# Marking the slots of a node: a clamp on GpSimd and an equality on VectorE in place of a distance on ScalarE and a comparison

## The chip, the cores and the metric

The kernel runs on one core of a Trainium2 chip. The metric is the device time of one launch in microseconds (us). Before the change the median of three runs is 543.99 us (543.93 to 545.51).

## The reference

One layer of a message-passing network over 128 graphs of 64 nodes with 128 features each. The adjacency matrix of a graph is symmetric, has ones on its diagonal and is sparse otherwise.

```python
f_i, f_j = x[:, :, None, :], x[:, None, :, :]                 # all pairs of nodes of a graph
m   = mlp(concat(f_i, f_j), msg weights)                      # 3 layers, relu and layernorm twice
agg = sum(m * adj[..., None], axis=2)
out = x + mlp(concat(x, agg), upd weights)                    # 3 layers, relu and layernorm twice
# mlp: h = layernorm(relu(x@w0 + b0)); h = layernorm(relu(h@w1 + b1)); return h@w2 + b2
```

## The kernel before

**Edges, not pairs.** Only pairs with an edge are worked on. Two graphs form a pair `p` (64 of them) whose nodes fill the 128 partitions; each graph gets `CAP` = 640 slots, one for each of its edges, in the order of the nodes. Four pairs form a block `b` (16 of them). Ten chunks of 512 edges go with a block, 160 in all.

**Node marks, the part that is changed.** A node of the pair (a partition) owns the slots from its start to its end, both running counts of edges. `place` (`place_first` for block 0) works out the counts: `before` is the start, `cum` the end, `mid` their sum. `slot` is a constant row 1, 3, 5, ... 1279 in 16-bit floats, so that a slot belongs to a node where |slot - mid| is less than the node's degree `deg`. Two functions make the marks: `distance(p)` writes `D[p]`, the absolute difference, on ScalarE, and `make_tp(p)` compares it with `deg` on VectorE and writes `TP[p]`, a matrix of 0 and 1, 128 x 640, in 16-bit floats. `D` has two buffers, `TP` eight. `node_rows(p)` widens `TP[p]` to 32 bits (on GpSimd from pair 6 on), `marks` and `compare` make a second matrix for the other end of each edge, `stack` puts both into `S` by DMAs of SP's queue, and `node_marks` turns `TP[p]` by another DMA.

**The edge layers.** For chunk `n`, `layer0(n)` gathers the first layer's sums by TensorE: the one-hot matrix `S` against the rows `ab` of the nodes, which are held as a high and a low part, so each piece takes two matmuls. A chunk of 512 slots overlaps one or two graphs of 640 slots: `pieces(n)` gives pieces of 512; 128 and 384; 256 and 256; 384 and 128; 512 in turn, in the order of the slots. ScalarE applies relu. `stats0` transposes the chunk into a PSUM bank (`hT`) and VectorE takes its statistics by bn_stats. `seed(n)` writes bias times standard deviation into the PSUM bank `z` of the chunk (two banks, `n % 2`), on VectorE for chunks with `n % 10` in 3, 4, 8 and on ScalarE in four pieces otherwise; `layer1(n)` adds its matmuls onto it, ScalarE applies relu, and `stats1` takes statistics again. `weights` (GpSimd) and `reduce` (TensorE) sum the edges of each node.

**The update.** Once in a block a `Unit` does the second mlp on 512 nodes. `bias0(u)` makes its first bias, `deg * c2u + ub0b`, by four VectorE instructions of 128 columns; `residual` (`xo`) and `upd_shift` (`usdb`) are GpSimd's, `layer_out` and `finish` VectorE's.

**Order.** It is written out by hand. `at(n, place, fn, ...)` files a step under iteration `n` and a place in it; the last loop runs the iterations, in each the places "a", "m", then layer 1, layer 0 and the transposes, "k", `stats1`, and the places "x" to "e". Each engine works its own instructions strictly in that order. Layer 1 of chunk `m` is in iteration `m + 8`. For pair `p`, whose slots begin in chunk `n = 2.5 p`, the distance is filed under `n - 7`, `make_tp` under `n - 6`, `node_rows` under `n - 5`, `stack` under `n - 4`. `bias0` is filed under the first iteration of its unit, four iterations ahead of its use by `layer_out`. The first three pairs are made before the loop, `distance(0)` between `place_first` and `place_pair(0)`.

Of the kernel before, what the change touches and what calls it, by code (L numbers as in the profile page):

```python
# [9 lines left out]
F32 = mybir.dt.float32  # L10
F16 = mybir.dt.float16
F32R = mybir.dt.float32r
I32 = mybir.dt.int32
AF = mybir.ActivationFunctionType
ALU = mybir.AluOpType
# [9 lines left out]
def tile_gnn(  # L25
# [40 lines left out]
    nc = tc.nc  # L66
    B, N, C = x.shape
    P = 128
    assert C == P and N == 64
    CAP = 640  # L70
# [9 lines left out]
    PB = 4  # L80
# [84 lines left out]
    slot = const.tile([P, CAP], F16, name="slot")  # L165
# [9 lines left out]
    W = {}  # L175
# [62 lines left out]
    def bc(t, n, axis=1):  # L238

        s = [P, n, C] if axis == 1 else [P, C, n]  # L240
        return t.unsqueeze(axis).to_broadcast(s)
# [60 lines left out]
    def edge_path(es):  # L302
        adp = es.enter_context(tc.tile_pool(name="adp", bufs=2))
        tpp = es.enter_context(tc.tile_pool(name="tpp", bufs=8))
# [35 lines left out]
        def at(n, place, fn, *args):  # L340
            plan.setdefault((n, place), []).append((fn, args))

        def run(n, place):
            for fn, args in plan.pop((n, place), ()):
                fn(*args)

        blocks = {b: {} for b in range(NB)}
        TP, S, H, ST0, V0, Y, ST1, Q, OH, WT, YS, MK, D, IR, JR, SR, Z = ({} for _ in range(17))
# [38 lines left out]
        def whole(b, eng):  # L387
            cum = cumall[:, b * PB:(b + 1) * PB]
            eng.tensor_scalar(cum, blocks[b].pop("raw"), WHOLE, WHOLE, op0=ALU.add,
                              op1=ALU.subtract)  # L390
            return cum
# [6 lines left out]
        def place(b):  # L398

            blk = blocks[b]  # L400
            cum = whole(b, nc.gpsimd)
            before = adp.tile([P, PB], F32, name="before")
            nc.gpsimd.tensor_tensor(before, cum, blk["deg"], op=ALU.subtract)
            blk["mid"] = adp.tile([P, PB], F32, name="mid")
            nc.gpsimd.tensor_tensor(blk["mid"], cum, before, op=ALU.add)
            pos = adp.tile([P, PB, N], F32, name="pos")
            nc.gpsimd.tensor_tensor(pos, blk.pop("rk"),
                                    before.unsqueeze(2).to_broadcast([P, PB, N]), op=ALU.add)
            blk["pos"] = pos
# [9 lines left out]
        def place_first():  # L419
            blk = blocks[0]  # L420
            rk = blk["rk"]
            cum = whole(0, nc.vector)
            before = blk["before"] = adp.tile([P, PB], F32, name="before")
            nc.vector.tensor_tensor(before, cum, rk[:, :, N - 1], op=ALU.subtract)
            blk["mid"] = adp.tile([P, PB], F32, name="mid")
            nc.vector.tensor_tensor(blk["mid"], cum, before, op=ALU.add)

        def place_pair(q):
            blk = blocks[0]
            for g in range(2):  # L430
                s = slice(g * N, (g + 1) * N)
                nc.vector.scalar_tensor_tensor(posall[s, 0, q, g, :], blk["rk"][s, q],
                                               blk["before"][s, q:q + 1], blk["an"][s, q],
                                               op0=ALU.add, op1=ALU.mult)
# [61 lines left out]
                del blk["ab_ps", half]  # L496


        def distance(p):
            b, q = divmod(p, PB)  # L500
            D[p] = tpp.tile([P, CAP], F16, name="d", bufs=2)
            nc.scalar.activation(D[p], slot, AF.Abs, bias=blocks[b]["mid"][:, q:q + 1], scale=-1.0)  # L502

        def make_tp(p):

            b, q = divmod(p, PB)
            tp = tpp.tile([P, CAP], F16, name="tp")
            nc.vector.tensor_scalar(tp, D.pop(p), blocks[b]["deg"][:, q:q + 1], None,
                                    op0=ALU.is_lt)
            TP[p] = tp  # L510

        def node_rows(p):
            IR[p] = tpp.tile([P, CAP], F32R, name="i32", bufs=2)
# [30 lines left out]
        def pieces(n):  # L544

            at_, end = n * CH * P, (n + 1) * CH * P
            while at_ < end:
                g, e = divmod(at_, CAP)
                w = min(end - at_, CAP - e)
                yield g, e, at_ - n * CH * P, w  # L550
                at_ += w

        def layer0(n):

            ps = ps_h.tile([P, CH * P], F32, name="hps")
            for g, e, c, w in pieces(n):
                s = S[g // 2][:, g % 2, e:e + w]
                for k, ab in enumerate(blocks[g // (2 * PB)]["ab", g // 4 % 2]):
                    nc.tensor.matmul(ps[:, c:c + w], lhsT=ab[:, g % 4, :], rhs=s,  # L559
                                     start=(k == 0), stop=(k == 1))  # L560
            H[n] = hp.tile([P, CH * P], F32, name="h")
            nc.scalar.activation(H[n], ps, AF.Relu, bias=b0c)  # L562
# [120 lines left out]
        def wide(name, u):  # L683

            if name not in u.blk:
                u.blk[name] = updp.tile([P, PB, C], F32, name=name,
                                        bufs=2 if name in ("uo", "xo", "m0") else 1)
            return u.blk[name][:, u.q, :]
# [6 lines left out]

        def bias0(u):
            u.m0 = wide("m0", u)
            for q in range(u.n):
                nc.vector.scalar_tensor_tensor(
                    u.m0[:, q, :], W["c2u"], u.blk["deg"][:, u.k0 + q:u.k0 + q + 1], W["ub0b"],  # L700
                    op0=ALU.mult, op1=ALU.add)

        def residual(u):
            u.xo = wide("xo", u)
# [103 lines left out]
        for b in reversed(range(NB)):  # L808
            o = b * CPB
            n = o + QC + SC  # L810
# [35 lines left out]
        for p in range(NP):  # L846
            n = p * TG * 2 // CH
            if p > 1:
                if p > 2:
                    at(max(n - 7, p - 2), "x" if p == PB + 1 else "a", distance, p)  # L850
                    at(max(n - 6, p - 2), "m", make_tp, p)
                at(n - 5, "x" if p == PB else "a", node_rows, p)
                at(n - 4, "a", stack, p, 0, IR)
                for k in range(2):
                    at(n - 5 + k, "k", marks, p, k)
                    at(n - 5 + k, "k", compare, p, k)
                at(n - 3, "a", stack, p, 1, JR)
            w = p // 2 * QC + QC + L1 + p % 2
            last = p // 2 == NQ - 1
            at(w - 4, "a", node_marks, p)  # L860
            q, h = divmod(p, 2)
            for g in range(2):
                wait = 3 if q == NQ - 3 else 2 if q == NQ - 2 else 2 + (2 * h + g + 1) // 2
                at(*((NCHK + L1, "b") if last else (q * QC + QC + L1 + wait, "e1")), weights, p, g)
            at(*((NCHK + L1 - 1, "x") if q == NQ - 3 else
                 (NCHK + L1 + 1 if last else q * QC + SC - (q == NQ - 2), "x1")), reduce, p)
        for q in range(NQ):
            n = q * QC + QC if q else LEAD
# [38 lines left out]
        turn_x_out(0, 0, 2)  # L907
        degrees(0)
        place_first()
        distance(0)  # L910
        place_pair(0)
        make_tp(0)
        place_rest()
        rows(0, 0, 0, 2)
# [4 lines left out]
        def marks_here(p):  # L919

            S[p] = sp.tile([P, 2, CAP], F32R, name="s")
            marks(p, 0)
            marks(p, 1, lambda: zbank(p % 2))
# [4 lines left out]
        def compare_here(p, g):  # L928
            s = slice(g * N, (g + 1) * N)
            for k in range(2):  # L930
                c = slice(k * HC, (k + 1) * HC)
                nc.vector.tensor_tensor(S[p][N:P, g, c], MK[p, k][s, 0:HC], cmpt[s, c],
                                        op=ALU.is_equal)
            if g:
                MK.pop((p, 0)), MK.pop((p, 1))
# [4 lines left out]
        rows_here(0, 0)  # L940
        rows_here(0, 1)
        compare_here(0, 0)
        distance(1)
        layer0(0)
        keep_busy(4)
        compare_here(0, 1)
        make_tp(1)
        distance(2)
        marks_here(1)
        layer0(1)  # L950
        keep_busy(4)
        rows_hi(0, 0, 2, 4)
        rows_here(1, 0)
        rows_here(1, 1)
        compare_here(1, 0)
        rows_lo(0, 0, 2, 4)
        layer0(2)
        keep_busy(2)
        make_tp(2)
# [96 lines left out]
    with ExitStack() as es:  # L1056
        es.enter_context(tc.manual_schedule())
        flag = edge_path(es)
# [160 lines left out]
```

## Time and profile before

The profiled execution took 544.21 us; its span, from the first to the last instruction, is 542.4 us, and 1.8 us lie around it.

| engine | busy, us | share of the span | instructions |
|---|---|---|---|
| TensorE matmul | 520.0 | 96% | 5513 |
| TensorE weight load | 471.6 | 87% | 5513 |
| VectorE (DVE) | 472.3 | 87% | 1271 |
| ScalarE (ACT) | 475.0 | 88% | 1108 |
| GpSimd (POOL) | 207.4 | 38% | 419 |

The TensorE clock was granted at 0.996 of full speed. Matmuls are pipelined and one that waits in the pipeline counts as busy, so TensorE's share says where it has work, not that it runs at its peak. One fp32 matmul stands in the records as two. A group of instructions is printed as: line, engine, operation, output<-inputs, shapes, count, then busy time and mean duration in ns, then the idle time of the engine before them and what ended it. "L508" is line 508 of the kernel before.

### The profile page before, as it was taken

Reading aid. Unit: us, or ns where it says so; the run is one execution under the profiler, and the core shown is the slowest. Engines: PE = TensorE matmul, PEld = TensorE weight load, DVE = VectorE, ACT = ScalarE, POOL = GpSimd, SP = SyncE. Lnnn points to the kernel's source line nnn. Section 1 sums busy time; section 2 is a strip of 40 time slices with the busy share of each in tenths; the row PEclk is TensorE's granted clock in tenths of the full one; section 3 lists DMA queues with packets and bytes.
Section 4 is the critical chain, followed back from the end, with each engine's and each line's share of the span. In section 5 each row is a group of like instructions: output and inputs, shape, how many; then the busy total and the mean of one; then the engine's idle time right before and its main releaser. Section 6 shows DMA issues by size and latency. Waiting matters only on the chain. (4 is left out here: it accounts for less than half of the span.)

```text
span 542.4 us, 15157 instructions
## 1 busy us (share of the span) xinstructions
PE 520.0 (96%) x5513; PEld 471.6 (87%) x5513; DVE 472.3 (87%) x1271; ACT 475.0 (88%) x1108; POOL 207.4 (38%) x419
## 2 busy tenths in 40 slices
PE   8989999999999999999999999999999999999784
PEld 7777889899898989989898989989999998988764
DVE  6759798998989899898989989898989989896745
ACT  6788999998989999898999989899999989887824
POOL 3103253525334363533435353443536254323230
PEclk9999999999999999999999999999999999999998
DMA  4456666545575665547464554557466445542101
GB/s 99 106 134 117 154 110 149 124 115 121 121 164 101 154 109 128 130 101 166 113 148 96 148 136 98 145 122 147 103 149 129 119 110 117 142 99 32 39 22 43
DMA packets 90762, 63.18 MB, mean 116 GB/s; under 512 B 57398, under 2 KB 74812, under 8 KB 90684
## 3 DMA queue, kind: packets, MB, share of 16 engines
q1 hardware_dynamic: 90396, 62.03, 51.3%
q8 instruction: 46, 0.75, 0.6%
q14 instruction: 32, 0.26, 0.1%
q10 hardware_dynamic: 288, 0.13, 0.1%
HBM read 6.82 MB, written 4.19 MB: 20 GB/s over the span
## 5 line engine op out<-in xcount | busy, mean ns | idle before, releaser
L614 PE MATMUL z<-w1c,h 128*128 128x128 f32 x1280 | 175.8, 280 | 5.2 <-DVE z L601 2.5
L614 PEld LDWEIGHTS z<-w1c,h 128*128 128x128 f32 x1280 | 155.6, 191 | 18.8 <-DVE z L601 8.6
L606 ACT ACTIVATE z<-b1b,m_sd 128x128 f32<-128x128 f32 x436 | 162.1, 372 | 10.7
L261 DVE BATCH_NORM_STATS2 st<-hT 128x6 f32<-128x256 f32 x320 | 118.8, 412 | 20.5 <-PE hT L568 18.3
L261 DVE BATCH_NORM_STATS2 st<-y 128x6 f32<-128x256 f32 x320 | 120.7, 418 | 4.2 <-ACT y L617 4.2
L617 ACT ACTIVATE y<-z 128x512 f32<-128x512 f32 x160 | 94.8, 593 | 20.6 <-PE z L614 19.1
L562 ACT ACTIVATE h<-hps,b0c 128x512 f32<-128x512 f32 x160 | 109.6, 685 | 3.2 <-PE hps L559 3.2
L568 PE MATMUL hT<-ident,h 128*128 128x128 f32 x640 | 97.5, 275 | 2.4 <-DVE st L261 1.3
L559 PE MATMUL hps<-s,abl 128*128 128x512 f32 (+3 forms) x256 | 91.9, 371 | 0.5 <-ACT s L926 0.4
L568 PEld LDWEIGHTS hT<-ident,h 128*128 128x128 f32 x640 | 73.7, 141 | 19.4 <-PE z L614 7.7
L650 POOL TENSOR_TENSOR w<-oh,m_q 128x192 f32<-128x192 f16 x126 | 61.5, 510 | 59.9 <-PE ma L711 25.9
L559 PE MATMUL hps<-s,abh 128*128 128x512 f32 (+3 forms) x256 | 78.0, 323 | 0.0
L517 POOL CAST i<-tp 128x640 fp32r<-128x640 f16 x58 | 41.7, 719 | 93.3 <-issue 47.9
L541 DVE TENSOR_TENSOR j<-mk,cmpt 128x320 fp32r<-128x320 f32 x124 | 58.5, 472 | 1.0 <-PE mk L533 1.0
L502 ACT ACTIVATE d<-slot,mid 128x640 f16<-128x640 f16 x64 | 52.8, 825 | 0.0
L559 PEld LDWEIGHTS hps<-s,abl 128*128 128x128 f32 x256 | 48.9, 191 | 3.6 <-ACT w2cT L200 2.0
L559 PEld LDWEIGHTS hps<-s,abh 128*128 128x128 f32 x256 | 48.9, 191 | 0.1
L665 PE MATMUL ys<-y,w 128*32 128x128 f32 x1488 | 47.0, 275 | 0.0
L665 PEld LDWEIGHTS ys<-y,w 128*32 128x32 f32 x1488 | 38.7, 110 | 4.1 <-issue 3.3
L493 DVE TENSOR_TENSOR abl<-mu,abh 128x512 fp32r<-128x512 f32 (+1 forms) x32 | 21.3, 664 | 22.9 <-ACT abh L487 22.9
L533 PE MATMUL mk<-tp,posall 128*128 128x320 f16 x126 | 37.7, 299 | 0.0
L279 POOL TENSOR_TENSOR m_v<-m_v,st 128x20 f32<-128x20 f32 x31 | 7.7, 250 | 78.3 <-DVE st L261 74.7
(204 smaller groups left out, 841.9 us busy)
## 6 DMA issues: line engine op xcount, KB each, us to landing
s<-i SPq DMA_DIRECT2D x124, 160.0 KB, 2.9
s<-j SPq DMA_DIRECT2D x124, 160.0 KB, 2.7
xn<-in_x_dram SPq DMA_DIRECT2D x15, 256.0 KB, 3.6
out_dram<-uo SPq DMA_DIRECT2D x15, 256.0 KB, 2.9
an<-in_adj_dram SPq DMA_DIRECT2D x16, 128.0 KB, 2.5
oh<-tp SPq DMA_TRANSPOSE x64, 3.3
xn<-in_x_dram SPq DMA_DIRECT2D x2, 128.0 KB
out_dram<-uo SPq DMA_DIRECT2D x2, 128.0 KB, 3.0
```

The lines of the kernel that those rows point to most:

```text
L261: nc.vector.bn_stats(st, src.rearrange("p t c -> p c t"))
L502: nc.scalar.activation(D[p], slot, AF.Abs, bias=blocks[b]["mid"][:, q:q + 1], scale=-1.0)
L517: nc.gpsimd.tensor_copy(IR[p], TP[p])
L541: nc.vector.tensor_tensor(JR[p][:, c], MK.pop((p, k))[:, 0:HC], cmpt[:, c], op=ALU.is_equal)
L559: nc.tensor.matmul(ps[:, c:c + w], lhsT=ab[:, g % 4, :], rhs=s, start=(k == 0), stop=(k == 1))
L562: nc.scalar.activation(H[n], ps, AF.Relu, bias=b0c)
L568: nc.tensor.transpose(ps[:, t, :], H[n][:, t * P:(t + 1) * P], ident)
L606: nc.scalar.activation(z[:, t, :], W["b1b"], AF.Copy, scale=SR[q][:, k + t:k + t + 1])
L614: nc.tensor.matmul(ps[:, t, :], lhsT=h[:, t * P:(t + 1) * P], rhs=W["w1c"], start=False, stop=True, skip_group_check=True)
L617: nc.scalar.activation(Y[n], ps, AF.Relu)
L650: (nc.vector if p == NP - 2 else nc.gpsimd).tensor_tensor(WT[p][:, g], oh, qs, op=ALU.mult)
L665: nc.tensor.matmul(YS[b][g * N + m * HN:g * N + (m + 1) * HN, k, :], lhsT=w[:, g, m, u, :], rhs=y, start=(u == 0), stop=(u == TH - 1), til ...
```

## The change

The half-open range of a node is clamped instead of measured. `place` and `place_first` write two small tiles, `lo` = 2 `before` and `hi` = 2 `cum`, where they wrote `mid`. `clamp(p)`, on GpSimd (on VectorE for pair 0), takes the place of `distance(p)`: `D[p]` is `slot` limited to `lo` and `hi`, which equals `slot` just where the slot belongs to the node. `make_tp` compares `D[p]` with `slot`, a tensor against a tensor, where it compared a tensor with a value of each partition. `bias0` becomes two GpSimd instructions over the whole unit. `layer0` takes the larger piece of a chunk first, which alters the order of chunks with `n % 5 = 1` (128 and 384) alone.

```diff
-            blk["mid"] = adp.tile([P, PB], F32, name="mid")
-            nc.gpsimd.tensor_tensor(blk["mid"], cum, before, op=ALU.add)
+            blk["ends"] = [adp.tile([P, PB], F32, name=v) for v in ("lo", "hi")]
+            nc.gpsimd.tensor_tensor(blk["ends"][0], before, before, op=ALU.add)
+            nc.gpsimd.tensor_tensor(blk["ends"][1], cum, cum, op=ALU.add)
...
-        def distance(p):
+        def clamp(p, eng=nc.gpsimd):
             b, q = divmod(p, PB)
             D[p] = tpp.tile([P, CAP], F16, name="d", bufs=2)
-            nc.scalar.activation(D[p], slot, AF.Abs, bias=blocks[b]["mid"][:, q:q + 1], scale=-1.0)
+            lo, hi = (v[:, q:q + 1] for v in blocks[b]["ends"])
+            eng.tensor_scalar(D[p], slot, lo, hi, op0=ALU.max, op1=ALU.min)
 
         def make_tp(p):
-            b, q = divmod(p, PB)
-            tp = tpp.tile([P, CAP], F16, name="tp")
-            nc.vector.tensor_scalar(tp, D.pop(p), blocks[b]["deg"][:, q:q + 1], None,
-                                    op0=ALU.is_lt)
-            TP[p] = tp
+            TP[p] = tpp.tile([P, CAP], F16, name="tp")
+            nc.vector.tensor_tensor(TP[p], D.pop(p), slot, op=ALU.is_equal)
...
-            for g, e, c, w in pieces(n):
+            for g, e, c, w in sorted(pieces(n), key=lambda v: -v[3]):
...
-            for q in range(u.n):
-                nc.vector.scalar_tensor_tensor(
-                    u.m0[:, q, :], W["c2u"], u.blk["deg"][:, u.k0 + q:u.k0 + q + 1], W["ub0b"],
-                    op0=ALU.mult, op1=ALU.add)
+            deg = u.blk["deg"][:, u.q].unsqueeze(2).to_broadcast([P, u.n, C])
+            nc.gpsimd.tensor_tensor(u.m0, bc(W["c2u"], u.n), deg, op=ALU.mult)
+            nc.gpsimd.tensor_tensor(u.m0, u.m0, bc(W["ub0b"], u.n), op=ALU.add)
...
-                    at(max(n - 7, p - 2), "x" if p == PB + 1 else "a", distance, p)
+                    at(max(n - 7, p - 2), "x" if p == PB + 1 else "a", clamp, p)
...
-        distance(0)
+        clamp(0, nc.vector)
...
-        distance(1)
+        clamp(1)
...
-        distance(2)
+        clamp(2)
```

More of the change, by code (lines that the diff above doesn't have):

```diff
@@ L424, in place_first @@
             nc.vector.tensor_tensor(before, cum, rk[:, :, N - 1], op=ALU.subtract)
-            blk["mid"] = adp.tile([P, PB], F32, name="mid")
-            nc.vector.tensor_tensor(blk["mid"], cum, before, op=ALU.add)
+            blk["ends"] = [adp.tile([P, PB], F32, name=v) for v in ("lo", "hi")]
+            nc.vector.tensor_tensor(blk["ends"][0], before, before, op=ALU.add)
+            nc.vector.tensor_tensor(blk["ends"][1], cum, cum, op=ALU.add)
         def place_pair(q):
```

## The prediction

> **What bounds the kernel now.** I read the busy shares first, then the same by stretches of 20 us, the groups by shape, the waits, and last the timeline of one block in the steady stage (215 to 277 us).
>
> ```profile
> PE 520.0 (96%) x5513; PEld 471.6 (87%) x5513; DVE 472.3 (87%) x1271; ACT 475.0 (88%) x1108; POOL 207.4 (38%) x419
> 220.00:240.00 20.00, 19.91 (x202) 17.76 (x201) 19.53 (x52) 18.80 (x44) 9.89 (x20) 1.00 0.47 111
> ```
>
> The second line is one stretch: PE, PEld, DVE, ACT and POOL busy. TensorE works without a hole, VectorE all but 0.5 us, ScalarE all but 1.2 us, GpSimd half. So three engines run level, and what taking work from one is worth depends on who is last at each point. The waits say who:
>
> ```profile
> PEld z L614 <- DVE z L601: 8.6, 31, 0.7
> DVE abl L493 <- ACT abh L487: 23.7, 17, 1.7
> ```
>
> TensorE waits for VectorE's seed (L601). From 90 to 464 us I find no wait for ScalarE over 60 ns on TensorE. VectorE's one regular wait is for `abh`, 1.4 us a time, once a block, and `abh` there waits for TensorE's `rows`. The timeline (start, duration) after that point:
>
> ```profile
> 220.90 1.04 POOL L748 TENSOR_TENSOR usdb<-bu1b,um_sd 128x512 f32<-128x512 f32 x1 [3.76 <-DMA s<-j]
> 221.01 1.11 DVE L508 TENSOR_SCALAR tp<-d,deg 128x640 f16<-128x640 f16 x1
> ...
> 222.04 0.75 DVE L261 BATCH_NORM_STATS2 st<-hT 128x6 f32<-128x256 f32 x2
> 222.18 0.72 POOL L517 CAST i<-tp 128x640 fp32r<-128x640 f16 x1 [0.25 <-DVE tp L508]
> ...
> 222.71 0.75 DVE L261 BATCH_NORM_STATS2 st<-y 128x6 f32<-128x256 f32 x2
> 223.38 0.68 DVE L601 TENSOR_TENSOR z<-b1b,m_sd 128x512 f32<-128x512 f32 x1
> 224.11 1.16 PE L614 MATMUL z<-w1c,h 128*128 128x128 f32 x8
> ...
> 229.87 0.74 DVE L261 BATCH_NORM_STATS2 st<-hT 128x6 f32<-128x256 f32 x2
> 230.75 0.63 PE L568 MATMUL hT<-ident,h 128*128 128x128 f32 x4
> ```
>
> VectorE is busy without a gap from `abl` (220.4) to past 230.6, and TensorE starts L614 and L568 just as L601 and L261 end. Counted from start to start of the matmuls, TensorE loses 0.14 us at 224.1 and 0.2 at 230.75, and again 0.15 at 237.8 (a bn_stats late) and 0.14 at 238.95 (a seed late): 0.63 us of a block of 31.2 us. I call these four points stalls 1 to 4. All are VectorE's. Before 3 and 4 stand the four `bias0` instructions (232.37 to 234.26), before 1 and 2 two `make_tp`.
>
> **What the skill says.** "SBUF — State Buffer", Who interferes with whom: VectorE and GpSimd share a port pair as an exclusive lock; a VectorE instruction in a 2-port mode, or with two SBUF inputs against a GpSimd one that reads SBUF, blocks the other for the whole instruction. The trace agrees: L508 takes 0.36 us alone and 1.11 when L748 is under way (13 times); L601 takes 0.68, and 0.78 the one time that it met a GpSimd tensor_tensor with 0.23 left; in 13 cases L601 came first and L389, 0.25 us alone, took 0.71. From these a blocked VectorE instruction ends later by what is left of the GpSimd one less about 0.13 (L601, L451) to 0.18 us (L508). "VectorE: DVE Perf Modes", The perf-mode tier table: a 16-bit tensor_scalar reaches 4x, a tensor_tensor 2x. The first fits L508's 0.36 us; the second isn't in this trace. "GPSIMD Engine Reference", Engine selection: one-input operations run at roughly line rate, two-input ones at half VectorE's speed.
>
> **The change, part by part.** The rows that it touches or leans on:
>
> ```profile
> L601 DVE TENSOR_TENSOR z<-b1b,m_sd 128x512 f32<-128x512 f32 x51 | 34.8, 682 | 0.0
> L508 DVE TENSOR_SCALAR tp<-d,deg 128x640 f16<-128x640 f16 x64 | 33.2, 519 | 1.0 <-ACT d L502 0.8
> L699 DVE SCALAR_TENSOR_TENSOR m<-c2u,deg,ub0b 128x128 f32<-128x128 f32 x64 | 28.1, 496 | 0.0
> L502 ACT ACTIVATE d<-slot,mid 128x640 f16<-128x640 f16 x64 | 52.8, 825 | 0.0
> L517 POOL CAST i<-tp 128x640 fp32r<-128x640 f16 x58 | 41.7, 719 | 93.3 <-issue 47.9 <-DVE tp L508 45.5
> L705 POOL TENSOR_TENSOR xo<-xn,cu2b 128x512 f32<-128x512 f32 x15 | 19.3, 1285 | 1.8 <-DVE uo L766 1.8
> L748 POOL TENSOR_TENSOR usdb<-bu1b,um_sd 128x512 f32<-128x512 f32 x13 | 13.5, 1042 | 47.4 <-DMA s<-j 25.9 <-ACT um_sd L269 21.4
> ```
>
> *ScalarE* loses 64 x 0.825 = 52.8 us. TensorE doesn't wait for it in the steady stage, so I put this at nothing there; what hides it is VectorE and TensorE, which stay as full. Once it shows: at 27.0 us VectorE waits 0.82 us for a distance, and TensorE for VectorE's next result (1.8 us idle before 28.53). That clamp is then long made: about -0.65.
>
> *VectorE* loses `bias0`, 4 x 0.5 = 2.0 us a block (28.1 in all). It stands ahead of stalls 3 and 4 with no idle time between, until `abl` meets `abh`. VectorE then reaches stall 3 some 0.8 us earlier, so 3 and 4 go: -0.29 a block. It does nothing for 1 and 2, since behind it lies the 1.4 us wait for `abh`.
>
> *make_tp* becomes a tensor_tensor of 640 elements. At 2x that is 320 cycles, as many as L541 spends on 320 fp32 elements in 0.472 us. So 0.475, 0.115 more than L508 alone. Behind L748 it stays blocked (two SBUF inputs) and ends some 0.15 later than now. Bounds: 0.36, and 0.81 if it runs at 1x.
>
> *clamp* is a GpSimd tensor_scalar of two operations on 640 elements; none of that size is in the trace. Below, the cast of 640 elements takes 0.72; above, the two-input rate of L748 ((1042 - 203) / 508 = 1.65 ns an element, 203 ns being a 128x4 one) gives 1.25. I take 0.95. Is it in time? I laid 61 clamps, two bias instructions a block (1.04 as L748, 1.29 as L705) and the `hi` into GpSimd's order and let each of its present instructions start no earlier than it did: every clamp ends at least 1.5 us ahead of its `make_tp`, 2.5 in the steady stage. `node_rows`, and behind it SP's queue of DMAs, moves by 0.3 at most, `weights` by 0.3; only `place_out` and a variance move by 2 to 3 us, and both are used two iterations (6 us) later. GpSimd goes from 207 to about 207 + 58 + 37 + 3 = 305 us, with room.
>
> The cost is in the lock. After a `make_tp` GpSimd does the cast at once (222.18 to 222.90) and now the clamp of the next pair directly behind it, from 0.78 to 0.78 + 0.95 = 1.73 us after the `make_tp` ended. VectorE does two pairs of bn_stats and starts L601 at 1.26. So L601 meets a clamp with 0.47 left and ends 0.47 - 0.13 = 0.34 later. The same pair of instructions stands before stall 4, where 0.8 us of slack has come from `bias0`. Before stalls 1 and 2 there's none: 0.15 (blocked `make_tp`) + 0.34 (L601) + 0.1 (second `make_tp`) = +0.6 a block. L451 will wait 0.6 for a bias instruction, in the stretch that `bias0` has left.
>
> *Larger piece first.* Chunks with 128 first take 0.66 us from their first matmul to the next operation, those with 384 first 0.60 where nothing waits (median and lower quartile of 32 each): the weights of a 128-column matmul load longer than it streams. 32 chunks x 0.05 = 1.6 us at most. Half of them lie between stalls 1 and 2, where VectorE sets the time: I count 0.05 a block.
>
> *The start.* The clamp of pair 0 lies on VectorE's path, where the distance ran beside `place_pair`: 0.36 + 0.17 for the extra `hi`, and the pair's first `make_tp` may be blocked by the clamp of pair 1; +0.5 to +1.1, +0.8 taken, against the -0.65.
>
> **Sum.** Steady: 0.6 - 0.29 - 0.05 = +0.26 over the 13 blocks that have L748: +3.4. The two blocks before (38 to 90 us), where VectorE is full and six seeds are late by 2.2 us together: some eight `make_tp`, half of them on the path, and a clamp or two in a seed's way, less block 0's bias: +0.7. Start +0.15. The tail (480 us on) has no distances, and its eight bias instructions stand where VectorE waits for ScalarE anyway: 0. In all +4.2 on 544.21 us, the profiled time (542.4 + 1.8); it lies 0.2 us over the median, so I give 548.0.
>
> **Rivals.** *(1) The same, but even.* With a clamp as short as the cast (0.72) L601 loses 0.11 instead of 0.34: 0.37 - 0.34 = nothing a block; 544.5 to 545. *(2) VectorE gains: faster.* If clamp and seed don't meet (the clamp is started before the bn_stats pair ends, or L601 isn't held), 0.25 - 0.34 = -0.09 a block, -1.2, with the start's -0.65 and early seeds no longer late by 0.6: 541.7. For it: 21 us less VectorE work in sum, and L601 hardly ever was held so far; against it: no GpSimd instruction stood there so far. It decides where the clamp takes under 0.6 us. *(3) make_tp at 1x* (0.81 us): +0.33 twice a block before stalls 1 and 2, 13 x 0.66 = +8.6: 556. *(4) GpSimd itself late*, needing clamps over 2.4 us: VectorE then waits at L508's place, over 560. *(5) ScalarE's 53 us shorten the time:* then TensorE would wait for L606 or L562 in the steady stage; it doesn't.
>
> **Numbers.** A run tells about 0.3% (1.6 us) from no change: faster is below 542.4, slower above 545.6. Forecast (clamp 0.8 to 1.3: 546 to 553) 0.53; (1) 0.17; (2) and (5) 0.20; (3) and (4) 0.10. The range 541.3 to 554 leaves out (3), (4) and a gain over 0.5%.
>
> **What would show it.** Right: L508's place at 0.47 alone; L601 at 1.0 instead of 0.68 in two of three cases, behind a GpSimd clamp; the wait of L614 for L601 longer in sum; no wait of `make_tp` for a clamp; ScalarE near 420 us with more idle time. Wrong: L601 still at 0.68 everywhere, waits of L614 for L601 gone, or a clamp that ends after VectorE is ready for it.

## The result: 1.35% slower, and the profile after

The kernel after takes 551.28 us, median of four runs (551.16 to 553.19), against 544.08 us for the kernel before on the same chip: a ratio of 1.0135 [1.0107, 1.0163]. The forecast was 548.0 us. The profiled execution took 551.16 us; its span grew from 542.4 to 549.4 us.

The busy shares of the kernel after, from its page, and then the same by stretches (length, then PE, PEld, DVE, ACT and POOL busy with counts, clock, DMA share, GB/s):

```profile
PE 515.1 (94%) x5513; PEld 471.2 (86%) x5513; DVE 473.8 (86%) x1209; ACT 436.2 (79%) x1044; POOL 415.6 (76%) x531
```

The stretch from 200 to 300 us, first after, then before:

```profile
200.00:300.00 100.00, 96.67 (x1087) 89.41 (x1087) 91.83 (x234) 84.04 (x201) 84.43 (x106) 1.00 0.57 128
```

```profile
200.00:300.00 100.00, 99.84 (x1109) 90.99 (x1107) 93.19 (x250) 93.08 (x215) 42.56 (x82) 1.00 0.55 126
```

TensorE, which had no hole, now stands still for 3.3 us in 100. ScalarE has 9 us less to do and GpSimd twice as much. VectorE, relieved of `bias0`, is as busy in sum as before, 473.8 against 472.3 us: its instructions became fewer and longer. Who makes TensorE wait is told by the waits of the kernel after (engine, line waited at, who ended the wait; us in sum, times, longest):

```profile
ACT y L617 <- PE z L614: 32.2, 58, 1.7
...
PE hT L568 <- DVE st L261: 10.8, 18, 0.9
...
PEld z L614 <- DVE z L601: 10.4, 21, 1.0
...
DVE tp L510 <- POOL d L505: 6.9, 13, 1.1
```

The line for L568 in the kernel before:

```profile
PE hT L568 <- DVE st L261: 1.3, 2, 0.9
```

TensorE's transposes wait 10.8 us in sum for bn_stats, where it was 1.3; its layer 1 waits 10.4 us for the seed, where it was 8.6. ScalarE waits for TensorE in turn (32.2 us in front of `y`). `make_tp` waits for a clamp 13 times. The groups that the change touches, first VectorE's and GpSimd's new ones, then `weights`, whose mean was 510 ns:

```profile
L505 POOL TENSOR_SCALAR d<-slot,lo,hi 128x640 f16<-128x640 f16 x63 | 158.1, 2511 | 0.4 <-issue 0.2
...
L510 DVE TENSOR_TENSOR tp<-d,slot 128x640 f16<-128x640 f16 x64 | 50.0, 781 | 7.0 <-POOL d L505 6.9
...
L601 DVE TENSOR_TENSOR z<-b1b,m_sd 128x512 f32<-128x512 f32 x51 | 40.6, 797 | 0.0
...
L650 POOL TENSOR_TENSOR w<-oh,m_q 128x192 f32<-128x192 f16 x126 | 71.3, 589 | 14.5 <-PE hT L568 5.3 <-PE ma L710 4.4 <-PE ys L665 3.8
```

**The clamp takes 2.51 us, not 0.95.** The seed (L601) went from 682 to 797 ns and `make_tp` (now L510) from 519 to 781 ns. How the long clamp reaches TensorE is seen in the block that the prediction walked through, in the timeline of the kernel after:

```profile
223.55 1.04 POOL L747 TENSOR_TENSOR usdb<-bu1b,um_sd 128x512 f32<-128x512 f32 x1 [3.22 <-DMA oh<-tp]
...
223.66 1.27 DVE L510 TENSOR_TENSOR tp<-d,slot 128x640 f16<-128x640 f16 x1
...
225.00 0.72 POOL L517 CAST i<-tp 128x640 fp32r<-128x640 f16 x1 [0.41 <-DVE tp L510]
...
225.70 2.50 POOL L505 TENSOR_SCALAR d<-slot,lo,hi 128x640 f16<-128x640 f16 x1
...
226.20 0.93 DVE L601 TENSOR_TENSOR z<-b1b,m_sd 128x512 f32<-128x512 f32 x1
...
227.04 0.26 DVE L290 RECIPROCAL m_q<-m_sq 128x20 f32<-128x20 f32 x1
...
227.18 1.16 PE L614 MATMUL z<-w1c,h 128*128 128x128 f32 x8 [0.23 <-DVE z L601]
...
228.17 1.89 POOL L650 TENSOR_TENSOR w<-oh,m_q 128x192 f32<-128x192 f16 x3
...
228.91 0.80 DVE L601 TENSOR_TENSOR z<-b1b,m_sd 128x512 f32<-128x512 f32 x1
...
229.62 0.79 DVE L510 TENSOR_TENSOR tp<-d,slot 128x640 f16<-128x640 f16 x1
...
234.36 0.63 PE L568 MATMUL hT<-ident,h 128*128 128x128 f32 x4 [0.66 <-DVE st L261]
```

The first three steps are the forecast's: `make_tp` is held by `usdb`, the clamp follows the cast, and the seed at 226.20 meets the clamp half a microsecond after its start and takes 0.93. The fourth step is not: the three `weights` instructions have their last input, `m_q` of L290, at 227.30, but stand behind the clamp in GpSimd's order and begin at 228.17, when it has ended. In the kernel before they began 0.13 us after that reciprocal, 1.5 us ahead of the second seed (225.84), and were over when it came:

```profile
224.37 1.44 POOL L650 TENSOR_TENSOR w<-oh,m_q 128x192 f32<-128x192 f16 x3 [1.47 <-PE ma L711]
```

Now they run beside the second seed (0.80 instead of 0.68) and the second `make_tp` (0.79; 0.38 in the kernel before), VectorE's next bn_stats are late, and L568 loses 0.66 at 234.36, which is stall 2.

### The profile page after: what moved, and what is told of

Same layout as the page of the kernel before. It is cut to its first block, busy times and chain, and to the rows that moved or that the text cites. A ratio compares the mean times of both kernels' runs of the same rounds, so it can differ in the third digit from the quotient of the medians.

```text
span 549.4 us, 15155 instructions
## 1 busy us (share of the span) xinstructions
PE 515.1 (94%) x5513; PEld 471.2 (86%) x5513; DVE 473.8 (86%) x1209; ACT 436.2 (79%) x1044; POOL 415.6 (76%) x531
## 4 chain that ended last, share of the span: by engine, by line
PE 56%; DVE 30%; issue 6%; ACT 5%; DMA 1%; POOL 1%; DVEq 0%; POOLq 0%; ACTq 0%
DVE st L261 14%; PE z L614 13%; PE hT L568 8%; PE ys L665 8%; PE hps L559 7%; PE mu L724 7%; DVE tp L510 5%; PE mu L475 5%; DVE z L601 3%; DVE j L541 3%; PE ma L710 2%; PE mk L533 2%; DVE uy L245 2%; ACT abh L489 1%; PE ys L894 1%
## 5 line engine op out<-in xcount | busy, mean ns | idle before, releaser
L614 PEld LDWEIGHTS z<-w1c,h 128*128 128x128 f32 x1280 | 155.6, 191 | 20.4 <-DVE z L601 10.4
L505 POOL TENSOR_SCALAR d<-slot,lo,hi 128x640 f16<-128x640 f16 x63 | 158.1, 2511 | 0.4 <-issue 0.2
L617 ACT ACTIVATE y<-z 128x512 f32<-128x512 f32 x160 | 95.3, 596 | 36.0 <-PE z L614 32.2
L568 PE MATMUL hT<-ident,h 128*128 128x128 f32 x640 | 98.0, 276 | 11.2 <-DVE st L261 10.8
L568 PEld LDWEIGHTS hT<-ident,h 128*128 128x128 f32 x640 | 72.0, 140 | 25.8 <-PE hps L559 12.7
L650 POOL TENSOR_TENSOR w<-oh,m_q 128x192 f32<-128x192 f16 x126 | 71.3, 589 | 14.5 <-PE hT L568 5.3
L559 PE MATMUL hps<-s,abh 128*128 128x512 f32 (+3 forms) x256 | 74.5, 322 | 0.0
L517 POOL CAST i<-tp 128x640 fp32r<-128x640 f16 x58 | 46.1, 795 | 24.7 <-DVE tp L510 11.6
L510 DVE TENSOR_TENSOR tp<-d,slot 128x640 f16<-128x640 f16 x64 | 50.0, 781 | 7.0 <-POOL d L505 6.9
L747 POOL TENSOR_TENSOR usdb<-bu1b,um_sd 128x512 f32<-128x512 f32 x13 | 13.5, 1042 | 40.2 <-ACT um_sd L269 30.6
```

The costliest lines, as they stand in the source:

```text
L505: eng.tensor_scalar(D[p], slot, lo, hi, op0=ALU.max, op1=ALU.min)
L510: nc.vector.tensor_tensor(TP[p], D.pop(p), slot, op=ALU.is_equal)
L568: nc.tensor.transpose(ps[:, t, :], H[n][:, t * P:(t + 1) * P], ident)
L614: nc.tensor.matmul(ps[:, t, :], lhsT=h[:, t * P:(t + 1) * P], rhs=W["w1c"], start=False, stop=True, skip_group_check=True)
L617: nc.scalar.activation(Y[n], ps, AF.Relu)
L650: (nc.vector if p == NP - 2 else nc.gpsimd).tensor_tensor(WT[p][:, g], oh, qs, op=ALU.mult)
```

## The experiments

To compare places and not only totals I took from each trace the time from the start of layer 1 of one chunk to that of the next, by the first chunk's number modulo 10 (its "place"), as a median over 12 blocks of the steady stage (chunks 20 to 139); "block" is the sum of the ten places. Place 2 holds stall 1, place 5 stall 2, and place 7 both stall 3 and stall 4. A layer 1 that had to wait for its seed needs 0.91 us to TensorE's next operation, where the same one takes 0.81 when the seed is early (chunk 8 before, and in `b_bias`), so that stalls 1 and 4 reach into places 3 and 8; there, too, lie the chunks that get the larger piece first. Places 0, 1, 4 and 6 hardly move in any kernel. All in us:

```
                     2      3      5      7      8      9     block
before             2.550  3.036  4.806  2.692  3.930  3.273  31.17
after              2.968  3.000  5.398  2.371  3.792  3.275  31.68
b_bias             2.547  3.036  4.798  2.368  3.826  3.287  30.75
b_piece            2.547  3.016  4.839  2.683  3.903  3.272  31.13
b_equal            2.709  3.034  4.922  2.787  3.929  3.272  31.53
a_marks            2.964  3.034  5.365  2.371  3.902  3.275  31.78
b_bias_piece       2.547  3.007  4.854  2.368  3.808  3.271  30.74
a_fill             2.716  3.002  4.965  2.371  3.792  3.275  31.00
a_fill_long        2.714  3.002  5.508  2.396  3.872  3.639  32.00
a_imm              2.914  3.002  5.501  2.371  3.793  3.275  31.73
a_one              2.800  3.004  5.003  2.370  3.796  3.274  31.13
b_bias_piece_root  2.378  2.923  4.848  2.368  3.808  3.271  30.48
a_root             2.366  2.922  5.278  2.370  3.793  3.275  30.88
b_root             2.378  2.943  4.814  2.689  3.932  3.270  30.89
```

### The parts, each alone

`b_bias` is the kernel before with the change's `bias0` and nothing else; `b_piece` has the larger piece first and nothing else. `b_equal` keeps ScalarE's distance and gives `make_tp` the changed kernel's form of instruction, so that it doesn't compute the right marks:

```diff
-            nc.vector.tensor_scalar(tp, D.pop(p), blocks[b]["deg"][:, q:q + 1], None,
-                                    op0=ALU.is_lt)
+            nc.vector.tensor_tensor(tp, D.pop(p), slot, op=ALU.is_equal)
```

`a_marks` is the kernel after with `bias0` and the order of the pieces set back, so that the marks are changed alone.

> The kernel before with the update's first bias alone moved to GpSimd. My theory: VectorE loses 2 us a block ahead of stalls 3 and 4, which go (0.29 us of a block; in the changed kernel the same stretch lost 0.46 with the piece order), so 538 to 540 us. Rival: the bias does not stand on the path, or its two GpSimd instructions hold the shared port against VectorE as long as VectorE is spared: 543.5 to 545 us.

> The kernel before with the larger gather piece first alone. My theory: 0.05 us a block, since the other of two chunks lies where VectorE sets the time: 543 to 543.5 us. Rival: the full 1.6 us of 32 chunks, 542.4 us; or nothing, 544 us.

> The kernel before with only make_tp's operation changed to the comparison of two tensors (D against slot; D is still the distance, so the marks are other ones). My theory: 0.12 us more for each make_tp alone and 0.17 behind usdb, on the path before stalls 1 and 2 (0.28 a block) and before 3 and 4 (0.1): 548 to 549.5 us. Rival: the comparison's length is not on the path and only the clamp costs: 544 to 545 us.

> The changed kernel without its bias and its piece order: clamp and equality alone. My theory: the loss before stalls 1 and 2 stays, and what bias and piece gave (0.46 us a block) is gone: 556 to 558 us. Rival: GpSimd's bias instructions are what makes GpSimd late, so that it gets better without them: 546 to 551 us.

| | median, us | before on the same chip | ratio |
|---|---|---|---|
| b_bias | 539.58 | 545.39 | 0.9901 [0.9875, 0.9926] |
| b_piece | 544.79 | 545.39 | 0.9991 [0.9978, 1.0005] |
| b_equal | 550.31 | 545.39 | 1.0117 [1.0087, 1.0147] |
| a_marks | 554.38 | 545.39 | 1.0163 [1.0143, 1.0184] |

The bias alone is a gain of 1%: places 7 and 8 lose 0.32 and 0.10, which are stalls 3 and 4. The order of the pieces can't be told from nothing; in the table it gains 0.02 and 0.03 at places 3 and 8 and loses 0.03 at place 5. The equality alone costs 0.16 and 0.12 at stalls 1 and 2 (and 0.10 at place 7, behind `bias0`). The marks alone cost 0.41 and 0.56 at stalls 1 and 2, but in all 9 us, not the 12 to 14 that were expected.

The parts do not add up. Alone they make -1.0, -0.1 and +1.6%, together +0.5%, and the change is +1.35%. The table says why: in `a_marks`, where `bias0` is still VectorE's, place 7 is 2.371 as well, and only place 8 keeps its length (3.90). Two things in its trace may account for it, which these runs do not part: TensorE comes a microsecond a block later, and the four bias instructions take 0.34 us each. In the kernel before the first two of them run beside GpSimd's `posall` (L416), and take 0.56 and 0.88; here the first two begin 2.1 us and more into a clamp, which doesn't hold them:

```profile
L699 DVE SCALAR_TENSOR_TENSOR m<-c2u,deg,ub0b 128x128 f32<-128x128 f32 x64 | 18.2, 344 | 0.0
```

(groups of `a_marks`). Once the marks have made TensorE late, moving the bias, with the order of the pieces, is worth some 0.1 us a block instead of 0.42.

### The clamp: its hold on VectorE, and its length

`a_fill` keeps the kernel after but lets GpSimd write ones into `D` where it clamped, without reading anything. `a_fill_long` writes `D` four times over by iota, so that GpSimd is occupied somewhat longer than by a clamp (2.87 us against 2.50), but also reads nothing. Neither computes the right marks.

```diff
         def clamp(p, eng=nc.gpsimd):
...
+            if eng is nc.gpsimd:                          # a_fill
+                nc.gpsimd.memset(D[p], 1.0)
+                return
...
+            if eng is nc.gpsimd:                          # a_fill_long
+                for _ in range(4):
+                    nc.gpsimd.iota(D[p], pattern=[[2, CAP]], base=1, channel_multiplier=0, ...)
+                return
```

> The changed kernel with each GpSimd clamp replaced by a memset of the same tile, which reads nothing and is short (the marks are other ones). My theory: what is left of the loss is the equality's, 0.16 us a block before stall 1 and 0.12 before stall 2, against 0.46 gained at stalls 3 and 4: 2 to 3 us below the kernel before, 541 to 542 of 544. Rival: the clamp is not the cause of the loss before stall 2 (0.59 us a block), the equality and the bias on GpSimd are: 547 to 551.

> The same with four iotas of the tile in place of the memset: GpSimd is busy about 2.6 us, as long as with the clamp, and reads nothing. It parts two costs of the clamp. My theory: before stall 2 the clamp's length is what costs, since the three weights instructions come later and meet the second seed and the second make_tp (0.48 us a block over a_fill); before stall 1 its lock costs (0.25), and that is gone here: a_fill + 6, 547 to 548 of 544. Rival: the lock is all: as a_fill. Second rival: the length is all: as the changed kernel, 551.

| | median, us | before on the same chip | ratio |
|---|---|---|---|
| a_fill | 540.58 | 545.28 | 0.9923 [0.9900, 0.9945] |
| a_fill_long | 554.65 | 545.28 | 1.0177 [1.0154, 1.0201] |

Groups of `a_fill`:

```profile
L506 POOL MEMSET d<- 128x640 f16 x63 | 39.8, 632 | 4.3 <-DVE tp L513 4.2
...
L513 DVE TENSOR_TENSOR tp<-d,slot 128x640 f16<-128x640 f16 x64 | 40.7, 635 | 0.1
...
L604 DVE TENSOR_TENSOR z<-b1b,m_sd 128x512 f32<-128x512 f32 x51 | 34.7, 681 | 0.0
```

With a short filling that reads nothing, the seed is back at 0.68 and the kernel is 0.8% under the one before: without the clamp no loss is left. What is left against `b_bias_piece` (below), 0.17 at stall 1 and 0.11 at stall 2, is the equality, as `b_equal` had it. No other place differs by more than 0.02 between these two kernels, although `b_bias_piece` has ScalarE's distances and `a_fill` has not: in the steady stage ScalarE's 53 us are worth nothing.

The timeline of `a_fill_long` parts the other two costs:

```profile
226.95 2.87 POOL L507 IOTA d<- 128x640 f16 x4
...
227.47 0.68 DVE L606 TENSOR_TENSOR z<-b1b,m_sd 128x512 f32<-128x512 f32 x1
...
229.78 2.14 POOL L655 TENSOR_TENSOR w<-oh,m_q 128x192 f32<-128x192 f16 x3
...
229.93 0.92 DVE L606 TENSOR_TENSOR z<-b1b,m_sd 128x512 f32<-128x512 f32 x1
...
230.76 0.79 DVE L515 TENSOR_TENSOR tp<-d,slot 128x640 f16<-128x640 f16 x1
```

The first seed starts 0.5 us into the iotas, as it did into the clamp, and takes its usual 0.68: place 2 stays at `a_fill`'s 2.71. So the 0.25 between 2.716 and 2.968 in the kernel after is the hold. But `weights` are at least as late as with the clamp (2.3 us behind the start of the first seed, where it was 2.0), the second seed and the second `make_tp` are held by them, and place 5 is 5.51. So it is GpSimd's length, without any hold by the filling itself, that makes the loss at place 5, which was 0.43 in the kernel after (5.398 against `a_fill`'s 4.965). `a_fill_long` loses 0.36 at place 9 too: its `make_tp` waits 14.0 us in sum for `D`, twice as long as in the kernel after. The kernel came out 9.4 us over the one before, where some 3.5 were expected; place 9 makes 12 x 0.36 = 4.3 of the difference.

### A shorter clamp

`a_imm` clamps between constants, `a_one` does only one operation; both read `slot` as the clamp does, and neither computes the right marks. Of `a_imm` there are only two runs.

```diff
+                eng.tensor_scalar(D[p], slot, 1.0, 1279.0, op0=ALU.max, op1=ALU.min)   # a_imm
+                eng.tensor_scalar(D[p], slot, 640.0, None, op0=ALU.max)                # a_one
```

> The changed kernel with the clamp's two limits as constants in place of a value of each partition (the marks are other ones): what makes the clamp 2.5 us long. If it is the two operations, 2.4 to 2.5 us and 551; if it is the values of the partitions, about 1 us, and then the total is near 544, the lock's 0.25 us a block over the kernel with the memset.

> The same with one operation (a maximum with a constant) in place of two. If the length comes by the operation: 1.3 to 1.6 us and 545 to 547; if the clamp's cost lies in the 16-bit elements or the instruction, 2.3 to 2.5 us and 551; if it runs as the cast does, 0.7 to 0.8 us and 543 to 544.

| | clamp, us | median, us | before on the same chip | ratio |
|---|---|---|---|---|
| a_imm | 2.35 | 552.97 | 545.23 | 1.0147 [1.0111, 1.0183] |
| a_one | 1.91 | 544.79 | 545.23 | 0.9978 [0.9957, 0.9999] |

The groups, `a_imm` first:

```profile
L506 POOL TENSOR_SCALAR d<-slot 128x640 f16<-128x640 f16 x63 | 148.2, 2353 | 5.3
```

```profile
L506 POOL TENSOR_SCALAR d<-slot 128x640 f16<-128x640 f16 x63 | 120.2, 1910 | 0.7 <-DVE tp L513 0.5
```

The second operation costs 0.44 us, the bounds of each partition 0.16; that one operation would take 1.3 to 1.6 us was wrong. The loss is steep between the two: place 5 is 5.00 with 1.91 us, 5.50 with 2.35, and 5.40 with the 2.51 of the kernel after. So not the length as such but the meeting decides, and the traces tell which meeting. The first seed (chunk 3), the second seed (chunk 4) and the second `make_tp` take 0.68, 0.68 and 0.48 us in `a_fill`. What they take longer in the other kernels, beside what places 2 and 5 have over `a_fill` (medians over the same blocks, us):

| | clamp or filling | first seed | place 2 | second seed, second `make_tp` | place 5 |
|---|---|---|---|---|---|
| after | 2.51 | +0.25 | +0.25 | +0.12, +0.31 | +0.43 |
| a_imm | 2.35 | +0.20 | +0.20 | +0.23, +0.31 | +0.54 |
| a_one | 1.91 | +0.08 | +0.08 | +0.05, 0 | +0.04 |
| a_fill_long | 2.87 | 0 | 0 | +0.24, +0.31 | +0.54 |

In each kernel place 2 is longer by what the clamp holds the first seed, and place 5 by what `weights` hold the two instructions behind it. With 1.91 us the second `make_tp` is not held at all.

### Away from `usdb`

`b_bias_piece` joins the two parts that don't touch the marks. Three more kernels move what holds `make_tp` at stall 1: the unit's `upd_root0` (`um_sd`) and `upd_shift` (`usdb`), filed under the eighth entry of `STEADY`, come one iteration earlier, in `b_bias_piece`, in the kernel after (`a_root`) and in the kernel before (`b_root`).

```diff
-        STEADY = (1, 1, 2, 3, 4, 7, 8, 6, 8, 9, 12, 13, 11, 14, 15)
+        STEADY = (1, 1, 2, 3, 4, 7, 8, 5, 8, 9, 12, 13, 11, 14, 15)
```

> The kernel before with the bias on GpSimd and the larger piece first, the node marks left as they were. My theory: the gains of b_bias (0.43 us a block at stalls 3 and 4) and b_piece add up: 1.0 to 1.2% below the kernel before, 537.5 to 538.5 of 544. Rival: the piece order gives nothing more: as b_bias.

> b_bias_piece with the update's first root, and with it usdb, filed one iteration earlier (STEADY's eighth entry 5 in place of 6), so that usdb ends before the make_tp that it blocked. My theory: that make_tp takes 0.36 instead of 1.11 us, stalls 1 and 2 (0.34 us a block) go: 4 us below b_bias_piece, 533 to 535 of 544. Rival: usdb then meets another VectorE instruction, or ScalarE's earlier root waits for the statistics: as b_bias_piece or above.

> The changed kernel with the update's first root filed one iteration earlier, so that usdb ends before the make_tp behind it. My theory: that make_tp falls from 1.27 to 0.48 us, and all of it is on VectorE's run before stalls 1 and 2: about 0.6 to 0.8 us a block, 8 to 10 us below the changed kernel, 541 to 543 where the kernel before takes 544. Rival: GpSimd, now 76% busy, sets the time by then and not VectorE's run: 548 to 551.

> The kernel before with that one entry alone. My theory: stalls 1 and 2 (0.34 us a block) go, stalls 3 and 4 lie behind bias0 and mostly stay: 4 us below the kernel before, 539 to 541 of 544. Rival: it only helps together with the moved bias: 543 to 544.

| | median, us | before on the same chip | ratio |
|---|---|---|---|
| b_bias_piece | 539.01 | 545.28 | 0.9884 [0.9863, 0.9906] |
| b_bias_piece_root | 534.49 | 545.28 | 0.9809 [0.9786, 0.9832] |
| a_root | 542.48 | 545.23 | 0.9940 [0.9924, 0.9956] |
| b_root | 542.96 | 545.23 | 0.9956 [0.9940, 0.9972] |

The timeline of `b_bias_piece_root`:

```profile
213.01 1.04 POOL L747 TENSOR_TENSOR usdb<-bu1b,um_sd 128x512 f32<-128x512 f32 x1 [0.48 <-ACT um_sd L269]
...
217.63 0.38 DVE L508 TENSOR_SCALAR tp<-d,deg 128x640 f16<-128x640 f16 x1
...
218.39 0.76 DVE L261 BATCH_NORM_STATS2 st<-hT 128x6 f32<-128x256 f32 x2 [0.38 <-PE hT L568]
```

`usdb` is over at 214.05, long before `make_tp`, which falls from 1.11 to 0.38, and the bn_stats after it wait for TensorE instead of the reverse. That is worth 0.17 at place 2 and 0.09 at place 3, the whole of stall 1. Stall 2 was expected to go as well, and stays (place 5 is 4.81 in `b_root`, 4.85 here): it does not come from `usdb`, and `b_root` gained 2.3 us instead of the 4 that were expected. `b_bias_piece_root` is the fastest version here, 1.9% under the kernel before, with the marks left to ScalarE. With the changed marks the same edit wins more (0.60 at place 2, stall 1 and the hold together), but ends 0.6%, not 1.9%, under the kernel before: place 5 is still 5.28. There the second seed isn't held any more (0.68), but the second `make_tp` is, by 0.31, and 0.31 is what place 5 has over `a_fill`.

## Why the prediction was right, and where not

**Direction and mechanism held.** ScalarE's distances were worth nothing in the steady stage: its instructions lost 52.2 us in sum, its idle time in front of `y` grew instead. (Its busy time fell to 436.2 us and not to the 420 that were named, since instructions that overlap count once there.) The loss came where it was put, at stalls 1 and 2, by VectorE instructions held beside GpSimd. Of a block's three seeds, though, the clamp held one and not two: the first takes 0.93, the second 0.80 because of `weights`, and the third stays at 0.69.

**The sum, term by term** (us a block):

| term | predicted | measured |
|---|---|---|
| `make_tp` held by `usdb` | +0.15 | 1.11 to 1.27, +0.16 |
| seed held by the clamp | +0.34 | +0.25 |
| second `make_tp`, own length | +0.1 | +0.11 |
| clamp's length: `weights` late | not in the sum | +0.43 |
| order of the pieces, at place 5 | not in the sum | +0.03 to +0.05 (`b_piece`, `b_bias_piece`) |
| stalls 1 and 2 in all | +0.6 | 2.968 - 2.550 + 5.398 - 4.806 = +1.01 |
| stalls 3 and 4 | -0.29 | -0.32 - 0.14 = -0.46 (places 7 and 8) |
| larger piece first | -0.05 | -0.04 (place 3) |
| sum | +0.26 | +0.51 |

Some 0.03 of the -0.14 at place 8 are the larger piece's, as `b_piece` has them. Outside the steady stage: layer 1 begins 0.13 us later (predicted 0.15), the two early blocks add 0.6 (0.7), and the rest after the twelve blocks adds 0.2 (0). Twelve blocks of 0.5 are 6.0, in all +7.0 us of span against +4.2.

**The step that failed** is the clamp's size: "I take 0.95", between bounds of 0.72 and 1.25. A cast and a two-input instruction were taken as the ends for an operation that was neither, and 2.51 lies at twice the upper one. From it followed two more wrong steps. "`weights` by 0.3": they begin up to 0.9 us later than their inputs allow, and that takes them into the second seed and the second `make_tp`, which is the 0.43 above. And GpSimd's "305 us": it is 415.6, most of the difference being 63 x (2.51 - 0.95) = 98 us.

**Where luck helped.** The hold on the seed came out near its value because two errors offset each other: the clamp ran far longer than was taken, and held VectorE far shorter than it ran (see the last section). With 2.51 us the prediction's own rule would have had the seed end 0.78 + 2.51 - 1.26 - 0.13 = 1.90 us later. And the total lies in the 546 to 553 that were forecast for a clamp of 0.8 to 1.3 us, which this clamp is not; the 0.43 that the sum lacked was in part made up by the 0.17 more that stalls 3 and 4 gave.

**"No wait of `make_tp` for a clamp" was wrong too**, 13 waits of up to 1.1 us. They stand at place 8, one in a block, and eleven of them are of some 0.47 us. Neither place 8 nor place 9 is longer than in `a_fill`, where this `make_tp` waits for nothing (3.792 and 3.275 in both), so that these eleven cost nothing. So rival (4)'s condition, a clamp of over 2.4 us, came true and its price did not; its 560 counted a wait as a loss without asking who waits next. Rival (1) needed a clamp of 0.72; but even `a_one`, at 1.91, is about level with the kernel before. Rival (3) is out: alone, the equality takes 0.48 us. Rival (2)'s gain needed seed and clamp not to meet; `a_fill`, where a short filling doesn't hold the seed, gains 0.8%. Rival (5) is out by the comparison of `a_fill` with `b_bias_piece`.

**The bias was given the credit for more than it did.** -0.29 was forecast for stalls 3 and 4 and -0.46 came, but `a_marks` has the part of place 7, -0.32, without the bias. On GpSimd alone the bias won 0.42 a block (`b_bias`).

**Open.** Why a GpSimd tensor_scalar needs this long is not shown, nor what in `a_marks` takes away place 7's loss. A clamp that stands behind `weights` in GpSimd's order was not tried, nor a clamp of one operation together with `usdb` moved away.

## What to carry to other kernels

Before an operation goes to an idle engine, measure that operation at that size there: rows of other operations bounded nothing here. Then lay out what stands behind it in that engine's order and ask whom those instructions will meet when they start later; the long clamp cost more by the `weights` that it pushed than by the seed that it held. And judge parts alone and together: the bias was a gain of 1% alone, and worth a quarter of that once another part had moved the same stall.

## What the hardware showed that I had not expected

- **A GpSimd tensor_scalar of this size is slow.** 640 16-bit elements of each partition took 1.91 us with one operation, 2.35 with two, 2.51 with bounds of each partition, where a cast of as many took 0.72 and a memset 0.63. That differs from what the Trainium skill says of one-input operations ("GPSIMD Engine Reference", Engine selection: roughly line rate); here the measurement decides.
- **It holds VectorE only at its start.** In the kernel after, the first seed of a block began 0.49 us into a clamp and ended 0.25 late. In `a_root` the same seed begins 0.86 us into a clamp that still has 1.6 us to run, and takes its usual time in all 12 blocks:

```profile
222.48 2.50 POOL L505 TENSOR_SCALAR d<-slot,lo,hi 128x640 f16<-128x640 f16 x1
...
223.33 0.69 DVE L601 TENSOR_TENSOR z<-b1b,m_sd 128x512 f32<-128x512 f32 x1
```

  With the 0.13 us by which a held instruction ends early, the hold would last to about 0.49 + 0.25 + 0.13 = 0.87 us, an estimate from these numbers. The third seed of `a_marks` fits it: it began 0.43 us into a clamp and ended 0.31 late. With constant bounds the same estimate gives 0.40 + 0.20 + 0.13 = 0.73 in `a_imm` and 0.51 + 0.08 + 0.13 = 0.72 in `a_one`: the second operation, 0.44 us of length, added nothing to the hold. "SBUF — State Buffer", Who interferes with whom, has the hold last for the whole instruction; for `usdb` the traces agree with it, for this instruction they don't.
- **A filling that reads nothing holds nobody**: the first seeds, which met memset or iota alone, kept their 0.68 us.
